# Windowed attention in a three-block kernel: attention weights turned in 32x32 blocks on VectorE and moved by transfers, the second tile's exponential with its row sum taken from PSUM, and a new order table

## The chip, the cores and the metric

The kernel runs on one core of a Trainium2 chip. The metric is the device time of one execution in microseconds (us); lower is better. Five instruction queues work side by side: PE (TensorE, matrix products and transposes; PEld is its weight load), DVE (VectorE), ACT (ScalarE), POOL (GpSimd) and SP (SyncE, which issues the transfers). Each queue runs its own instructions in the order in which they were written, and waits for the others through semaphores. TensorE's results land in PSUM, from which DVE and ACT read; everything else lies in SBUF, 128 partitions wide.

## The reference

The input is 16 sequences of 256 tokens with 128 channels. Four residual blocks follow each other: a state-space scan, a two-layer feed-forward block with local attention, a power attention, and the same feed-forward block once more.

```python
x = L0_attn_a_resid
x = x + scan_block(layernorm(x))
x = x + ffn_block(layernorm(x))
x = x + power_block(layernorm(x))
x = x + ffn_block(layernorm(x))
```

The change is in the feed-forward block. Each of its two layers is this, for each sequence (8 heads of 64, window of 64 tokens; a token sees its own window and the one before):

```python
h = shift_token(x)
q, k, v = split(h @ wqkv)              # to heads
q, k = l2norm(q) * qs, l2norm(k) * ksc
q, k = rotary_xpos(q, k)
sim = (8 * q) . k                      # per window, 64 queries by 128 keys
sim = where(mask, -max, sim)
attn = softmax(sim)
x = x + (attn . v) @ wo
h = layernorm(shift_token(x)) * lg + lb
a, g = split(h @ w1 + b1)
x = x + (a * gelu(g)) @ w2 + b2
```

## The kernel before, in words

All values are 32-bit floats. After the scan block (`ssm_block`), three blocks share one arena of SBUF (`mem`) and one set of PSUM banks: `ffn_block(1, ...)`, `power_block`, `ffn_block(3, ...)`. A block is a list of small steps, each with a place on one line of time: the place is counted in units of a planned length (39.2 for one turn of the feed-forward table, 20.5 for the power block's). At the end of `tile_hybrid_kernel` the three lists are laid one behind the other, where `ahead` says by how many units a block begins before the end of the one in front, sorted by place, and the steps are called in that order. Every engine is wrapped in `Pinned`, which keeps an engine's instructions in the written order; as all of them are issued from its one line, the profile gives L88 to nearly everything, and groups are told apart by tiles and shapes.

The feed-forward block has N = 32 sequence passes (two layers of 16 sequences), two in a group, so 16 groups. `period` is the order table of one turn: a word such as `we0.1:4` is the step `we` (weigh) on tile 0 of the second sequence of the group that entered 4 turns ago. A word without a point is a step of the whole group, in the feed-forward half of the layer (names with U). In one turn all steps of two sequences are issued once, each at its own lag.

The attention of one sequence, by steps (t is the tile of 128 queries; a is 0 for queries, 1 for keys; r is the half of the heads):

- `p`, `sq`, `ro`, `ss`, `ra`: queries and keys are projected (PE), squared (ACT), multiplied by the rotary tables (DVE), square-summed (DVE), and the two rotary parts added (`rotated`, POOL, two additions of half the width).
- `b`, `i`, `nw`: inverse norms `rn` (POOL and ACT). `no` (`normed`, POOL) multiplies q and k by them, four times a sequence.
- `t`, `tc`: queries and keys turned by PE, copied by ACT into `qkT`.
- `k` (`mask`, ACT) writes the band of 0 and -1e30 into a pair of PSUM banks, `s` (`scores`, PE) adds the products to it, `mx` (`maxima`, DVE) takes the row maxima of the 8 heads, `lm` (`less_maximum`, DVE) writes the difference to `pr` in SBUF and gives the pair back, `e` (`exponentials`, ACT) takes the exponential of 128 x 1024 in one instruction, `su` (`sums`, DVE) sums the rows and inverts, `wo` (`weights_of`, POOL) multiplies.
- `wt` (`turn_weights`, PE) turns the weights in four 128x128 transposes for each half into a PSUM bank, `wc` (`turned_weights`, ACT) copies the bank to `prT`, `we` (`weigh`, PE) multiplies the values by them.
- `oc`, `mi`, `ma`: the result is copied (ACT), multiplied by `wo` (PE) and added (DVE). After the second tile `ma` issues three transfers on SP, which write the token-shifted rows (`mem<-u_all`). `vc` (`values_out`) copies the values and issues two transfers on SP of 64 rows of 2 KB (`mem<-mem`), which make the copy of the values shifted by half a tile.

The feed-forward half of a group: `Us`, `Uf`, `Un` (layer norm), `Ut`, `Uc` (turned), `Ur` (six products with w1), `Ug` (three Gelu, with two loads of ACT's tables), `Um` (three products on DVE), `Ub`, `Ud` (w2), `Ua` (sum).

FFN_LATE names the buffers in the arena: a word count and how many of each. Attention weights have three `pr` and two `prT` buffers of 1024 words for each partition.

Of the kernel before, what the change touches and what calls it, by code (L numbers as in the profile page):

```python
# [20 lines left out]
P = 128  # L21
# [15 lines left out]
QK_SCALE = 8.0  # L37
MASKED = -1e30


# [5 lines left out]
def kernel(ctx: ExitStack, tc: tile.TileContext, io, out: bass.AP):  # L46
# [615 lines left out]
    NP = HEADS // 2  # L662
    HF = DH // 2
    NC = len(hidden_chunks())

    def ffn_weights(fw):
# [6 lines left out]
        for t in range(2):  # L673
            m = const.tile([P, P], F32, name=f"band{t}")
            pool.memset(m, 0.0)
            for w in range(t + 1):
                q0 = w * WINDOW
                part = m[q0 : q0 + WINDOW] if t else m

                for sign, base in ((1, 0), (-1, WINDOW)):  # L680
                    pool.affine_select(
                        out=part, in_=part, pattern=[[-sign if t == 0 else sign, P]],
                        compare_op=ALU.is_ge, fill=MASKED, base=base,
                        channel_multiplier=sign if t == 0 else -sign,
                    )
            bands.append(m)
# [55 lines left out]

    FFN_LATE = [("rn", 32, 2), ("qkT", 2048, 2), ("vx", 1536, 4), ("pr", 1024, 3), ("prT", 1024, 2), ("oT", 512, 2)]
    FFN_LATE += [("mx", 8, 4), ("rl", 8, 4), ("shifted0", 512, 1), ("shifted1", 512, 1), ("hn", 512, 1)]
    FFN_LATE += [("hnT", 512, 1), ("hid", 1536, 1), ("ub", 512, 1)]
    FFN_LATE += [(f"ln_{x}4", 4 * n, 4) for x, n in (("st", 6), ("mv", 2), ("r", 1), ("mr", 1))]

    def ffn_block(k, fw, store, shared):
# [112 lines left out]
        def rotated(n, q, t, a):  # L861
            m2 = q.pop(("m2", t, a))
            m = q["m", t, a] = sb.tile([P, HEADS, DH], F32, name=f"f{k}_m_{n}_{t}_{a}", tag="m", bufs=8)
            for x, y in ((slice(0, HF), slice(HF, DH)), (slice(HF, DH), slice(0, HF))):
                pool.tensor_add(m[:, :, x], m2[:, 0, :, x], m2[:, 1, :, y])
            sb.free(m2)
# [37 lines left out]
        def normed(n, q, t, a):  # L904
            m = q["m", t, a]
            pool.tensor_mul(m, m, q["rn"][:, t, a, :].unsqueeze(2).to_broadcast([P, HEADS, DH]))
            sb.free(q["rn"], 4)

# [50 lines left out]


        def maxima(n, q, t):
            mx = q["mx", t] = sb.tile([P, 2, NP], F32, name=f"f{k}_mx_{n}_{t}", tag="mx", bufs=4)
            dve.tensor_reduce(mx, q["sim", t], AX.X, ALU.max)

        def less_maximum(n, q, t):
# [4 lines left out]
        def exponentials(n, q, t):  # L970
            pr = q["pr", t]
            act.activation(pr, pr, AF.Exp)

        def sums(n, q, t):
            rl = q["rl", t] = sb.tile([P, 2, NP], F32, name=f"f{k}_rl_{n}_{t}", tag="rl", bufs=4)
            dve.tensor_reduce(rl, q["pr", t], AX.X, ALU.add)
            dve.reciprocal(rl, rl)
# [4 lines left out]

        def turn_weights(n, q, t, r):
            pr = q["pr", t]
            ppt = bank(q, ("ppt", t, r), [P, NP, P], f"f{k}_ppt_{n}_{t}_{r}")
            for p in range(NP):
                pe.transpose(ppt[:, p, :], pr[:, r, p, :], ident)
            sb.free(pr, 2)


        def turned_weights(n, q, t, r):
            if r == 0:
                q["prT", t] = sb.tile([P, 2, NP, P], F32, name=f"f{k}_prT_{n}_{t}", tag="prT")
            act.copy(q["prT", t][:, r], give_back(q, ("ppt", t, r)))

        def weigh(n, q, t):

            prT, vx = q.pop(("prT", t)), q["vx"]
            po = bank(q, ("po", t), [P, NP, P], f"f{k}_po_{n}_{t}")
            for p in range(NP):  # L1000
                for w in range(t + 1):
                    qs = slice(w * WINDOW, (w + 1) * WINDOW) if t else slice(0, P)
                    for r in range(2):
                        pe.matmul(
                            po[r * DH : (r + 1) * DH, p, qs], vx[:, 2 - w if t else 0, 2 * p + r, :],
                            prT[:, r, p, qs], start=True, stop=True,
                        )
            sb.free(prT)
            sb.free(vx, 2)
# [93 lines left out]
        def unit_sum(g, q):  # L1103
# [12 lines left out]
            nw=newton, no=normed, t=turn, tc=turned, k=mask, s=scores, mx=maxima, lm=less_maximum,  # L1116
            e=exponentials, su=sums, wo=weights_of, wt=turn_weights, wc=turned_weights, we=weigh,
            oc=weighed, mi=mix, ma=mixed, Us=unit_stats, Uf=unit_factors, Un=unit_norm, Ut=unit_turn,
# [3 lines left out]
        period = """  # L1122
            ns.0:0 Uf:5 p00.0:2 e1.1:4 ma0.0:4 ro01.0:2 t11.0:3 s0.0:3 tc11.0:3 ro11.1:3 oc1.0:4
            v0.0:2 sq00.0:2 su1.1:4 ra11.1:3 Ud0:6 vc0.0:2 Un:5 mx0.0:3 t10.0:3 wt00.1:4 ss00.0:2
            tc10.0:3 wt01.1:4 lm0.0:3 wc00.1:4 Ud1:6 ra01.0:2 wc01.1:4 i.1:3 mi1.0:4 n.0:1 wo1.1:4
            p11.0:2 ma1.0:4 Ua:6 v1.0:2 ro00.0:2 nw.1:3 sq11.0:2 k1.0:3 p10.0:2 ss01.0:2 ra00.0:2
            vc1.0:2 p00.1:2 ro11.0:2 Ut:5 no00.1:3 s1.0:3 Uc:5 no01.1:3 e0.0:3 we0.1:4 mx1.0:3
            ra11.0:2 sq10.0:2 nf.1:1 oc0.1:4 ut.0:1 wt10.1:4 ss10.0:2 wt11.1:4 lm1.0:3 wc10.1:4
            Ur10:5 uc.0:1 wc11.1:4 Ur11:5 ss11.0:2 e1.0:3 ro10.0:2 b.0:2 we1.1:4 no11.1:3 k0.1:3
            su0.0:3 ra10.0:2 t00.1:3 oc1.1:4 v0.1:2 tc00.1:3 su1.0:3 no10.1:3 t01.1:3 vc0.1:2  # L1130
            p01.1:2 sq00.1:2 wo0.0:3 Ur12:5 tc01.1:3 ss00.1:2 sq01.1:2 ro00.1:2 mi0.1:4 i.0:2 Ug:5
            wo1.0:3 s0.1:3 ma0.1:4 ro01.1:2 mi1.1:4 nw.0:2 Ur01:5 ma1.1:4 mx0.1:3 ra00.1:2 p10.1:2
            ss01.1:2 t10.1:3 Ub:5 sq10.1:2 Um1:5 t11.1:3 tc10.1:3 v1.1:2 lm0.1:3 tc11.1:3 no00.0:2
            wt00.0:3 vc1.1:2 wt01.0:3 no01.0:2 ss10.1:2 ns.1:0 wc00.0:3 p01.0:1 ro10.1:2 wc01.0:3
            no11.0:2 Ur00:5 k1.1:3 ra01.1:2 wt11.0:3 Um0:5 e0.1:3 wt10.0:3 Us:4 we0.0:3 n.1:1
            ra10.1:2 wc10.0:3 sq01.0:1 s1.1:3 oc0.0:3 su0.1:3 wc11.0:3 ut.1:1 p11.1:2 mx1.1:3
            wo0.1:3 Ur02:5 uc.1:1 Um2:5 t00.0:2 t01.0:2 no10.0:2 tc00.0:2 lm1.1:3 we1.0:3 sq11.1:2
            tc01.0:2 nf.0:0 mi0.0:3 ss11.1:2 k0.0:2 b.1:2
        """
# [372 lines left out]
    for block, length, ahead in (  # L1512
        (ffn_block(1, fw, False, shared), 39.2, 0.0), (power_block(w, dram, shared), 20.5, 60.0),
        (ffn_block(3, fw, True, shared), 39.2, 20.0),
    ):
        begin, work = block
        start = end - ahead
        line.append((start, begin, ()))
        line += [(start + at * length, step, args) for at, step, args in work]
        end = max(at for at, *_ in line)  # L1520
# [55 lines left out]
```

## Time and profile before

| what | value |
|---|---|
| median of 3 runs | 2166.41 us (2164.24 to 2166.89) |
| span of the profiled execution | 2164.0 us |
| mean granted TensorE clock in it | 0.982 |
| PE busy, share of the span | 2027.4 us, 94% |
| PEld | 1327.1 us, 61% |
| DVE | 1846.0 us, 85% |
| ACT | 1709.8 us, 79% |
| POOL | 1892.6 us, 87% |

Busy times are unions over the instructions of an engine; matmuls are pipelined and their ends modelled, so PE's busy time says that products follow each other without a gap, not that each runs at its peak. Successive instructions of ACT and DVE overlap a little, so a duration is longer than the distance from one start to the next; the distance is what a queue pays.

The chain that ended last, by engine: PE 55%, POOL 17%, DVE 9%, ACT 9%, issue 7%, the rest SP, DMA and queues. Some of the groups of the whole execution, by shape (busy us, mean ns of one):

| group | count | busy us | mean ns |
|---|---|---|---|
| PE transposes, bank<-ident,mem 128x128 (feed-forward and power block) | 3104 | 424.9 | 277 |
| ACT copies, mem<-bank 128x512 | 976 | 535.9 | 594 |
| ACT, mem<-mem 128x1024 (exponentials) | 224 | 238.2 | 1067 |
| DVE, mem<-pair,mem 128x1024 (less_maximum) | 128 | 155.6 | 1216 |
| DVE, sums mem<-mem 128x8 of 128x1024 | 128 | 152.8 | 1194 |
| POOL, mem<-mem 128x256 (rotated) | 512 | 360.6 | 729 |
| POOL, mem<-mem 128x512 | 320 | 329.5 | 1043 |

### The profile page before, as it was taken

To read this page: it belongs to the slowest core of one execution; us is meant where nothing else is said; L and a number is where in the kernel's file an instruction comes from. 1 tells how busy PE (TensorE), PEld (TensorE's weight loads), DVE (VectorE), ACT (ScalarE), POOL (GpSimd) and SP (SyncE) were. 2 spreads that over 40 slices of the span, in tenths; PEclk is the share of its full clock that TensorE was granted. 3 is DMA by queue.
4 is the path that set the end of the run, shared out by engine and by line. 5 is a ranking of instruction groups with operands and counts; after the bars stand their busy time and mean duration, and the time that the engine had idled before them with its cause. 6 is when DMAs were issued, how large, how long until landed. Compare 5 with 4: busy or idle time off the path is not lost.

```text
span 2164.0 us, 44300 instructions
## 1 busy us (share of the span) xinstructions
PE 2027.4 (94%) x16184; PEld 1327.1 (61%) x16184; DVE 1846.0 (85%) x3291; ACT 1709.8 (79%) x2879; POOL 1892.6 (87%) x2177
## 2 busy tenths in 40 slices
PE   6999999877999999999988999998899999999997
PEld 2344444334667677777765777775567777777775
DVE  3999999998988888888856999997988888888883
ACT  5777777746888887878866999997788887878874
POOL 6899999968999888888967999996999988888993
PEclk8999999999999999999997999999999999999999
DMA  3322322211110110111103323220010111101110
GB/s 100 98 84 78 103 80 77 83 44 24 24 23 16 23 24 18 22 23 23 23 11 118 112 87 119 105 95 8 21 23 17 23 23 24 23 16 33 28 28 23
DMA packets 96837, 104.35 MB, mean 48 GB/s; under 512 B 50818, under 2 KB 62956, under 8 KB 96620
## 3 DMA queue, kind: packets, MB, share of 16 engines
q1 hardware_dynamic: 95932, 101.37, 16.5%
q8 instruction: 128, 2.10, 0.4%
q14 instruction: 89, 0.73, 0.1%
q10 hardware_dynamic: 688, 0.15, 0.0%
HBM read 73.72 MB, written 2.62 MB: 35 GB/s over the span
## 4 chain that ended last, share of the span: by engine, by line
PE 55%; POOL 17%; DVE 9%; ACT 9%; issue 7%; SPq 1%; DMA 1%; POOLq 0%; DVEq 0%; ACTq 0%
PE bank L88 44%; POOL mem L88 7%; PE pair L88 7%; POOL bx L88 7%; DVE mem L88 6%; ACT mem L88 4%; DVE hs L88 2%; ACT pair L88 2%; SPq L88 1%; POOL hs L88 1%; ACT a L88 1%; DMA mem<-u_all 1%; PE xe_ps L88 1%; PE y_ps L88 1%; POOL sf L88 1%
## 5 line engine op out<-in xcount | busy, mean ns | idle before, releaser
L88 POOL TENSOR_TENSOR mem<-mem 128x256 f32<-128x256 f32 (+5 forms) x1328 | 1157.0, 901 | 88.0 <-DVE mem L88 66.2
L88 ACT COPY mem<-bank 128x512 f32<-128x512 f32 (+4 forms) x1152 | 592.4, 558 | 145.3 <-PE bank L88 139.9
L88 PEld LDWEIGHTS bank<-ident,mem 128*128 128x128 f32 x3104 | 352.4, 141 | 171.1 <-issue 105.3
L88 PE MATMUL bank<-ident,mem 128*128 128x128 f32 x3104 | 424.9, 277 | 15.7 <-POOL mem L88 11.0
L88 PE MATMUL bank<-wqkv,mem 128*128 128x512 f32 x768 | 384.8, 606 | 1.8 <-ACT mem L88 1.8
L88 DVE TENSOR_REDUCE mem<-mem 128x8 f32<-128x512 f32 (+1 forms) x384 | 325.9, 849 | 9.6 <-ACT mem L88 9.2
L88 DVE TENSOR_TENSOR mem<-bank,rope 128x1024 f32<-128x1024 f32 x256 | 309.1, 1217 | 25.1 <-POOL mem L88 16.6
L88 POOL TENSOR_TENSOR bx<-dx,bb 128x1024 f32<-128x1024 f32 x126 | 295.0, 2364 | 15.6 <-DVE dx L88 10.9
L88 DVE TENSOR_TENSOR_SCAN hs<-a,bx 128x1024 f32<-128x1024 f32 x128 | 291.7, 2284 | 14.0 <-ACT a L88 12.2
L88 ACT ACTIVATE mem<-mem 128x1024 f32<-128x1024 f32 (+2 forms) x384 | 281.0, 737 | 25.0 <-DVE mem L88 16.7
L88 PE MATMUL pair<-mem 64*64 64x128 f32 (+2 forms) x4096 | 256.6, 296 | 22.9 <-DVE mem L88 13.9
L88 PE MATMUL y_ps<-hs,ident 128*128 128x512 f32 x512 | 243.3, 600 | 11.0 <-DVE hs L88 6.5
L88 PEld LDWEIGHTS pair<-mem 64*64 64x64 f32 (+2 forms) x4096 | 194.7, 160 | 75.2 <-issue 27.7
L88 ACT ACTIVATE a<-delta,neg_a 128x510 f32<-128x510 f32 x256 | 176.3, 690 | 76.8 <-DVE hs L88 71.8
L88 ACT ACTIVATE mem<-bank 128x512 f32<-128x512 f32 (+1 forms) x272 | 160.9, 593 | 61.7 <-PE bank L88 57.8
L88 PE MATMUL bank<-mem 128*64 128x64 f32 (+2 forms) x4608 | 203.3, 255 | 5.4 <-ACT mem L88 2.9
L88 PEld LDWEIGHTS bank<-mem 128*64 128x64 f32 (+1 forms) x4608 | 156.8, 128 | 64.3 <-issue 30.0
L88 PE MATMUL bank<-mem,w 128*128 128x512 f32 x384 | 191.9, 598 | 3.8 <-ACT mem L88 3.8
L88 PEld LDWEIGHTS y_ps<-hs,ident 128*128 128x128 f32 x512 | 95.7, 190 | 148.7 <-issue 120.3
L88 DVE TENSOR_REDUCE mem<-pair 128x8 f32<-128x1024 f32 x128 | 153.3, 1198 | 30.3 <-PE pair L88 30.3
L88 PEld LDWEIGHTS bank<-wqkv,mem 128*128 128x128 f32 x768 | 128.6, 194 | 72.3 <-issue 60.7
L88 DVE TENSOR_TENSOR mem<-pair,mem 128x1024 f32<-128x1024 f32 x128 | 155.6, 1216 | 0.4
(135 smaller groups left out, 2830.4 us busy)
## 6 DMA issues: line engine op xcount, KB each, us to landing
bb<-repsd SPq DMA_DIRECT2D x128, 256.0 KB
mem<-pngd SPq DMA_DIRECT2D x64, 512.0 KB
mem<-mem SPq DMA_DIRECT2D x128, 128.0 KB
mem<-u_all SPq DMA_DIRECT2D x64, 64.0 KB
mem<-u_all SPq DMA_DIRECT2D x64, 63.5 KB
x_all<-in_resid_dram SPq DMA_DIRECT2D x8, 256.0 KB
out_dram<-x_all SPq DMA_DIRECT2D x8, 256.0 KB
wqkv<-in_wqkv_dram SPq DMA_DIRECT2D x6, 256.0 KB
```

What stands on the lines that cost most here:

```text
L88: bi = getattr(self.eng, name)(*args, **kw)
```

## The change

In the feed-forward block:

- The weights are no longer turned by PE and copied by ACT. DVE transposes each tile of weights in blocks of 32x32 (`turn_weights`, one instruction of 128 x 1024 for each tile) into a buffer `T`, ordered by block column. A block transpose leaves each block in its own 32 partitions, so a step `mv` (`move_weights`) issues 16 transfers on SP for each sequence, each of 32 partitions by 2 KB, which put the blocks where they belong, into `PT`. `weigh` reads `PT` in runs of 32 columns. `T` and `PT` hold both tiles of a sequence, two buffers of 2048 words each; `prT` is gone.
- For the second tile (RAW = (1,)) the queries aren't multiplied by their inverse norms. `maxima` multiplies the maxima by the negated norms, and 8 exponentials of 128 x 128 read the scores in PSUM, with the norm as scale, the scaled maximum as bias and the row sum as a second output; `less_maximum` and the sum on DVE fall away for this tile, and the pair of banks is given back after its exponentials. Its mask fill is -1e25 instead of -1e30.
- `rotated` is one addition of the whole width that reads its second part with the halves exchanged, instead of two of half the width.
- The order table is a new one: the steps stand in other places and at other lags. A turn's planned length is 35.6 units instead of 39.2, and the last block begins 60 units before the end of the power block instead of 20.

```diff
+FAR = -1e25
+RAW = (1,)
+QB = 32
...
+    NB = P // QB
+    NORMED = 3
...
-    FFN_LATE = [("rn", 32, 2), ("qkT", 2048, 2), ("vx", 1536, 4), ("pr", 1024, 3), ("prT", 1024, 2), ("oT", 512, 2)]
+    FFN_LATE = [("rn", 32, 4), ("qkT", 2048, 2), ("pr", 1024, 3), ("T", 2048, 2), ("vx", 1536, 4), ("PT", 2048, 2)]
...
-            for x, y in ((slice(0, HF), slice(HF, DH)), (slice(HF, DH), slice(0, HF))):
-                pool.tensor_add(m[:, :, x], m2[:, 0, :, x], m2[:, 1, :, y])
+            pool.tensor_add(
+                m.rearrange("p h (f d) -> p h f d", f=2), m2[:, 0].rearrange("p h (f d) -> p h f d", f=2),
+                m2[:, 1].rearrange("p h (f d) -> p h f d", f=2)[:, :, ::-1],
+            )
...
+        def query_norms(q):
+            return q["rn"][:, 1, 0].rearrange("p (c r) -> p r c", r=2)
+
         def maxima(n, q, t):
             mx = q["mx", t] = sb.tile([P, 2, NP], F32, name=f"f{k}_mx_{n}_{t}", tag="mx", bufs=4)
             dve.tensor_reduce(mx, q["sim", t], AX.X, ALU.max)
+            if t in RAW:
+                dve.scalar_tensor_tensor(mx, mx, -1.0, query_norms(q), ALU.mult, ALU.mult)
...
         def exponentials(n, q, t):
-            pr = q["pr", t]
-            act.activation(pr, pr, AF.Exp)
+            if t not in RAW:
+                pr = q["pr", t]
+                act.activation(pr, pr, AF.Exp)
+                return
...
+            for r in range(2):
+                for p in range(NP):
+                    act.activation(
+                        pr[:, r, p, :], sim[:, r, p, :], AF.Exp, bias=mx[:, r, p : p + 1],
+                        scale=norms[:, r, p : p + 1], accum_out=rl[:, r, p : p + 1],
+                    )
+            ps.give_pair_back(q, ("sim", t))
...
-        def turn_weights(n, q, t, r):
-            pr = q["pr", t]
-            ppt = bank(q, ("ppt", t, r), [P, NP, P], f"f{k}_ppt_{n}_{t}_{r}")
-            for p in range(NP):
-                pe.transpose(ppt[:, p, :], pr[:, r, p, :], ident)
-            sb.free(pr, 2)
-
-
-        def turned_weights(n, q, t, r):
-            if r == 0:
-                q["prT", t] = sb.tile([P, 2, NP, P], F32, name=f"f{k}_prT_{n}_{t}", tag="prT")
-            act.copy(q["prT", t][:, r], give_back(q, ("ppt", t, r)))
+        def turn_weights(n, q, t):
+            if t == 0:
+                q["T"] = sb.tile([P, NB, 2, HEADS, QB], F32, name=f"f{k}_T_{n}", tag="T")
+            dve.transpose(
+                q["T"][:, :, t],
+                sb.free(q.pop(("pr", t))).rearrange("p r c (b i) -> p b (r c) i", i=QB),
+            )
+
+
+        def move_weights(n, q):
+            turned_, dst = q.pop("T"), sb.tile([P, NB, 2, HEADS, QB], F32, name=f"f{k}_PT_{n}", tag="PT")
+            q["PT"] = dst
+            for b in range(NB):
+                for kb in range(NB):
+                    sp.dma_start(dst[kb * QB : (kb + 1) * QB, b], turned_[b * QB : (b + 1) * QB, kb])
+            sb.free(turned_)
...
+                    bs = slice(2 * w, 2 * w + 2) if t else slice(0, NB)
...
                         pe.matmul(
-                            po[r * DH : (r + 1) * DH, p, qs], vx[:, 2 - w if t else 0, 2 * p + r, :],
-                            prT[:, r, p, qs], start=True, stop=True,
+                            po[r * DH : (r + 1) * DH, p, qs].rearrange("d (b i) -> d b i", i=QB),
+                            vx[:, 2 - w if t else 0, 2 * p + r, :], PT[:, bs, t, r * NP + p, :],
+                            start=True, stop=True,
                         )
...
+            k0.1:3 mi1.0:4 sq10.1:2 ma1.0:4 Ur11:6 ut.0:1 vc0.0:2 v1.0:2 Us:5 tc10.1:3 vc1.0:2
+            Ur10:6 ra01.1:2 no01.0:2 no11.0:2 s0.1:3 Ur12:6 ro10.1:2 uc.0:1 Ug:6 tr0.0:3 p00.0:1
+            ss10.1:2 sq00.0:1 Ur01:6 no11.1:3 mx0.1:3 su1.0:3 no00.0:2 t00.0:2 t01.0:2 ra00.1:2
+            lm0.1:3 Um1:6 Uf:5 Ur00:6 wo1.0:3 p11.1:2 ns.0:0 nf.0:0 tc00.0:2 ro00.0:1 nf.1:1
+            tr1.0:3 mv.0:3 p01.0:1 t10.0:2 tc01.0:2 ra10.1:2 k0.0:2 sq11.1:2 ss11.1:2 ss00.0:1
+            e0.1:3 b.1:2 t11.0:2 tc11.0:2 n.0:0 s0.0:2 tc10.0:2 mx0.0:2 ra00.0:1 Um0:6 n.1:1
+            lm0.0:2 we0.1:4 t11.1:3 sq01.0:1 tc11.1:3 ro01.0:1 v0.1:2 i.1:2 k1.1:3 p10.0:1
+            we1.1:4 oc0.1:4 v1.1:2 Un:5 su0.1:3 nw.1:2 p11.0:1 ro11.1:2 s1.1:3 ra01.0:1 no01.1:2
+            ss01.0:1 ra11.1:2 ut.1:1 no00.1:2 mx1.1:3 oc1.1:4 vc0.1:2 e0.0:2 mi0.1:4 wo0.1:3
+            ma0.1:4 sq11.0:1 vc1.1:2 mi1.1:4 sq10.0:1 su0.0:2 uc.1:1 ma1.1:4 Ur02:6 Ub:6
+            ro11.0:1 ra11.0:1 p00.1:1 Um2:6 e1.1:3 ro10.0:1 k1.0:2 ss10.0:1 su1.1:3 ss11.0:1
+            ra10.0:1 we0.0:3 p01.1:1 Ud0:6 t00.1:2 oc0.0:3 sq00.1:1 tr0.1:3 Ut:5 Uc:5 tc00.1:2
+            s1.0:2 sq01.1:1 t01.1:2 b.0:1 wo1.1:3 ss00.1:1 tc01.1:2 we1.0:3 i.0:1 Ud1:6 oc1.0:3
+            mx1.0:2 e1.0:2 ro01.1:1 v0.0:1 t10.1:2 ro00.1:1 wo0.0:2 mi0.0:3 tr1.1:3 ns.1:0
+            mv.1:3 nw.0:1 ma0.0:3 p10.1:1 ss01.1:1 Ua:6
...
-        (ffn_block(1, fw, False, shared), 39.2, 0.0), (power_block(w, dram, shared), 20.5, 60.0),
-        (ffn_block(3, fw, True, shared), 39.2, 20.0),
+        (ffn_block(1, fw, False, shared), 35.6, 0.0), (power_block(w, dram, shared), 20.5, 60.0),
+        (ffn_block(3, fw, True, shared), 35.6, 60.0),
```

## The prediction

> **What bounds the kernel now.** I read the page first (span, busy slices), then the table of windows over single turns of the feed-forward loop, then the timelines of PE, DVE and SP inside one turn, and last the groups by shape.
>
> ```profile
> span 2164.0 us, 44300 instructions
> PE   6999999877999999999988999998899999999997
> ...
> ```
>
> PE is at nine tenths nearly everywhere, so the page alone doesn't tell the stages apart. By the names of the tiles the feed-forward blocks run from 490 to about 1130 us and from about 1500 to the end; the scan block before them and the power block between them keep their instructions. Inside a feed-forward block the trace repeats every 39.08 us, which is one turn of the table (two sequences). Columns: busy time of each engine, then granted clock, DMA share, GB/s.
>
> ```profile
> core 0: us, PE busy (x) PEld busy (x) DVE busy (x) ACT busy (x) POOL busy (x), PEclk, DMA share, GB/s
> 800.36:839.44 39.08, 39.08 (x359) 27.98 (x358) 33.59 (x49) 31.65 (x55) 33.71 (x45) 1.00 0.10 22
> 839.44:878.52 39.08, 39.08 (x359) 27.99 (x358) 33.61 (x49) 31.68 (x55) 33.70 (x45) 1.00 0.10 22
> ```
>
> PE never rests; DVE, POOL and ACT have 5.5, 5.4 and 7.4 us to spare. So a turn is PE's work, and each block has 16 turns plus a start and an end.
>
> ```profile
> 777.77 1.47 PE L88 MATMUL bank<-ident,mem 128*128 128x128 f32 x12
> 779.08 1.50 PE L88 MATMUL bank<-w,mem 128*128 128x128 f32 x12
> ...
> 773.39 2.35 DVE L88 TENSOR_TENSOR mem<-bank,rope 128x1024 f32<-128x1024 f32 x2
> ...
> 791.11 1.21 DVE L88 TENSOR_REDUCE mem<-mem 128x8 f32<-128x1024 f32 x1
> 792.35 0.20 DVE L88 RECIPROCAL mem<-mem 128x8 f32<-128x8 f32 x1
> 792.47 1.17 DVE L88 TENSOR_REDUCE mem<-mem 128x8 f32<-128x1024 f32 x1
> ```
>
> Prices from start to start: a transpose on PE (779.08 - 777.77) / 12 = 0.109 us; a 1024-element DVE operation 2.35 - 1.22 = 1.13; a sum with the reciprocal that waits for it 1.24 + 0.12.
>
> **The change, part by part, in one turn.**
>
> **PE.** turn_weights gives up 4 transposes for each of 2 tiles, 2 halves and 2 sequences: 32 x 0.109 = 3.49 us. weigh issues the same matmuls, but reads its moving side in pieces of 32 (four pieces, or two). The start of a matmul bounds a piece's price: 32 matmuls of 64 columns take 1.08 us, 16 of 128 take 1.02, so 0.004 us is left besides the columns; 160 extra pieces are at most 0.6 us, at least 0. I take 0: PE 39.08 - 3.49 = 35.6 (to 36.2).
>
> **ACT.**
>
> ```profile
> L88 ACT COPY mem<-bank 128x512 f32<-128x512 f32 x144 | 79.8, 592 | 18.5 <-PE bank L88 18.3
> L88 ACT ACTIVATE mem<-mem 128x32 f32<-128x32 f32 x24 | 5.8, 242 | 0.4
> L88 ACT ACTIVATE mem<-bank,lb,lg 128x512 f32<-128x512 f32 x6 | 4.7, 781 | 5.9 <-PE bank L88 5.9
> ...
> L88 ACT COPY mem<-bank 128x128 f32<-128x128 f32 x32 | 7.2, 291 | 0.0
> ```
>
> turned_weights goes: 8 copies at 0.49 from start to start (three take 1.57), 3.9 us. Two exponentials of 1024 elements go, at 0.95: 1.9. In come 16 exponentials of 128 elements from PSUM, with bias and scale columns and a row sum. The copy of that size takes 0.291, two columns cost 0.781 - 0.592 = 0.19: 0.48 each, or 0.37 where it overlaps the next by the 0.105 that the copies do. No row shows the row sum. Below: nothing, 0.37. Above: no overlap and a separate instruction like the smallest here, 0.48 + 0.24 = 0.72. I take 0.45, nearer to the lower end, as DVE's accumulator read (82 ns in the power block) lies under the next operation: 7.2 us. ACT 31.7 - 5.8 + 7.2 = 33.1 (31.9 to 37.4).
>
> **DVE.** The second tile loses its subtraction (2 x 1.13) and its sum (2 x 1.24), and gains a product of 8 elements that waits for the maximum, priced like the reciprocal (2 x 0.24): 29.3 us. Then 4 block transposes of 1024 elements. None is in the trace. Nearest are the one-pass operations of this size, 1.13; below, 0.68 as for a 512-element reduction; above, 2.28, the scan's price for 1024. I take 1.13: DVE 33.9 (32.1 to 38.5).
>
> **POOL.** The second tile's query scaling goes (2 x 0.95) and eight pairs of half additions become single ones (2 x 0.69 - 0.95 = 0.43 each): 33.7 - 5.3 = 28.4; if the reversed reading eats that gain, 31.8. It stays clear of the bound. The other fill value of the mask and the larger rn buffer issue nothing in the loop.
>
> **SP.** move_weights issues 16 transfers for each sequence, each 32 rows of 2 KB.
>
> ```profile
> 781.93 4.65 SPq L88 DMA_DIRECT2D mem<-u_all  x3
> 786.68 1.20 SPq L88 DMA_DIRECT2D mem<-mem  x2
> ...
> 764.08 1.80 SPq L88 DMA_DIRECT2D mem<-mem  x2
> ...
> q1 hardware_dynamic: 179, 0.27, 66.9%
> ```
>
> The nearest transfers are vx's (64 rows of 2 KB): 0.56 us each to issue, 0.61 apart, and once 1.15 (the 1.80 less 0.65), behind the u_all group. So 32 x 0.61 = 19.5 us, with the 2 x (4.65 + 1.2) that are there: 31.2 of 35.6 us. The last line is of the 1.7 us in which one such transfer moves: 0.669 x 1.7 x 16 / 128 rows = 0.142 us a row, so one move is 512 x 0.142 / 16 = 4.5 us of the DMA engines, less than its issue. A move lands about 16 x 0.61 + 2 = 12 us after the second block transpose. Queued behind it on SP are vc's, ma's transfers and the next move. By places in the new table the tightest run is tr1.1 (0.95 of a turn) to we0.0 (1.76): 0.81 x 35.6 = 28.8 us, in which SP must issue move 1 (9.8), ma1.0 (4.65), vc1.0 (1.2), move 0 (9.8) and land it (2): 27.5. That fits by 1.3 us. What is late when it doesn't is we0.0, and PE stands behind it.
>
> Here a rule speaks against the change. The Trainium skill (DMA: Bandwidth & Descriptors, Bandwidth) says to batch transfers to 1 MiB and gives 0.95 us for 64 KB, measured from HBM over the other path. Were that a time that each of 32 moves holds the queue, an estimate from that page is 30.4 us, and SP would need 42 us a turn, past today's 39.08; by the rows it needs 31.2.
>
> **Outside the turns.** The third block may start 40 table units earlier: at 1460 to 1500 us DVE leaves some 10 us idle and PE 8; I take -8 (0 to -15). Against it, all Ur, Ug and Um go from lag 5 to 6, past the last attention: one more chain of gate, product and fall at each block's end, half hidden under the power block; +8 (0 to +20). Together 0.
>
> **Sum.** PE's 35.6 stands against 33.9, 33.1 and 31.2 on engines that feed each other in order, 95, 93 and 88% full where they were 86, 81 and 30. I add 0.8 us of waits: 36.4 (a choice; 0 to 1.8). Gain 32 turns x (39.08 - 36.4) = 86 us. The profiled execution has a span of 2164.0; the median of the runs is 2166.4, 2.4 above. 2164 - 86 + 2.4 = 2080.
>
> **Rivals.**
> 1. A wait takes the old bound's place: SP's run tr1.1 to we0.0 fails by 2.5 us (a few issues at 1.15 instead of 0.56 do it, and they follow the u_all group as here). PE waits in every turn: 38.1, 2164 - 32 x 1.0 + 2 = 2135. For it: a margin of 1.3 us. Against: PT has two buffers and the table can slip.
> 2. DVE or ACT becomes the bound: block transposes at the scan's 2.28 give 38.5, 2164 - 18 + 2 = 2148; ACT at 0.72 gives 37.4, 2112. For it: neither operation is in the trace. Against: both lie at far ends.
> 3. Slower: SP's issue itself bounds the loop. From (39.08 - 11.7) / 32 = 0.86 us a transfer, gap included, it decides; at the 1.15 seen once and 0.06 between, 32 x 1.21 + 11.7 = 50.4 us a turn, 2164 + 32 x 11.3 + 2 = 2528. For it: one issue in four shown took that long. Against: that one stood behind 127-row transfers, and rows drain faster than they are issued.
>
> **Chances.** Forecast 0.55 (its own range 2045 to 2115: turns of 35.6 to 37.4, ends within 15 us); rival 1 0.14; rival 2 0.11; rival 3 0.15; about no change 0.05, where rivals 1 and 2 meet the old turn; of this, 0.02 is faster by more than 0.2% (4 us, about what a measurement of this kernel can tell from no change), 0.02 within it and 0.01 slower. Faster is 0.55 + 0.14 + 0.11 + 0.02 = 0.82, same 0.02, slower 0.16. The range for 8 in 10 reaches from 2040 (PE's full 111 us and the earlier start) to 2170, so that it takes in rivals 1 and 2; left out are rival 3 with the slower hundredth and some 0.03 below, 0.19.
>
> **What would show it.** A turn of 35.6 to 37 us with PE still full, and 32 fewer transposes in it, is the forecast. Block transposes near 1.2 us, small exponentials 0.4 to 0.5 us apart, DVE's and ACT's busy shares above 90%: steps right. PE idle before the first weigh of a sequence, released by a DMA: rival 1. DVE or ACT full and PE not: rival 2. SP issuing without a break, over 0.86 us each: rival 3. The forecast is wrong if a turn is over 37.4 us, or if the ends cost more than 20 us.

## The result, and the profile after

| | median | runs | profiled span | mean clock |
|---|---|---|---|---|
| before | 2166.65 us | 2164.24 to 2167.72 (4) | 2164.0 us | 0.982 |
| after | 2283.80 us | 2273.46 to 2287.44 (4) | 2278.9 us | 0.947 |

The ratio is 1.0538, with a 95% interval of 1.0512 to 1.0564: the changed kernel is 117 us slower, where 86 us of gain were forecast. It lies outside the range, on the other side.

The page of after first: span, PE's share in 40 slices, the chain that ended last, and the one group of PE that stands out (counts, busy us, mean ns, then idle time just before it and what ended most of that).

```profile
span 2278.9 us, 43705 instructions
...
PE   6999999868889899898868999998779899899877
...
PE 44%; POOL 12%; ACT 10%; DVE 10%; SPq 10%; issue 8%; DMA 5%; POOLq 0%; ACTq 0%; DVEq 0%
...
L91 PE MATMUL bank<-mem 128*64 128x64 f32 (+2 forms) x4608 | 225.7, 268 | 147.8 <-DMA mem<-mem 137.6
```

PE, at 9 throughout the loops before, is now at 8 in many slices. 137.6 us of its idle time stand before the products that read the moved weights (`weigh`), and a transfer ends them. SP's queue and the DMA, 1% each of the chain before, are 15% of it.

The windows over four turns of the first feed-forward block (columns as in the prediction):

```profile
core 0: us, PE busy (x) PEld busy (x) DVE busy (x) ACT busy (x) POOL busy (x), PEclk, DMA share, GB/s
760.00:800.90 40.90, 37.79 (x328) 25.53 (x327) 33.97 (x50) 32.41 (x76) 30.69 (x34) 0.96 0.30 72
...
841.80:882.70 40.90, 37.58 (x327) 25.48 (x326) 33.97 (x50) 32.41 (x76) 30.64 (x34) 0.96 0.30 72
```

A turn takes 40.9 us where it took 39.08, and no engine fills it: DVE, ACT and POOL have 7 to 10 us to spare, PE over 3, and PE's clock is 0.96. So the bound is a chain through several queues. It shows when the timelines of SP, PE and DVE over one turn are laid side by side. SP (start, time from the first of the run to the end of the last, how many issues):

```profile
849.00 10.06 SPq L91 DMA_DIRECT2D mem<-mem  x16
859.16 4.66 SPq L91 DMA_DIRECT2D mem<-u_all  x3
863.94 13.43 SPq L91 DMA_DIRECT2D mem<-mem  x20
877.47 4.60 SPq L91 DMA_DIRECT2D mem<-u_all  x3
889.88 2.46 SPq L91 DMA_DIRECT2D mem<-mem  x4
```

PE:

```profile
873.59 1.02 PE L91 MATMUL bank<-wqkv,mem 128*128 128x512 f32 x2
877.94 1.97 PE L91 MATMUL bank<-mem 128*64 128x128 f32 x16 [3.32 <-DMA mem<-mem]
...
883.84 1.10 PE L91 MATMUL pair<-mem 64*64 64x128 f32 x32
```

DVE:

```profile
885.01 1.22 DVE L91 TENSOR_REDUCE mem<-pair 128x8 f32<-128x1024 f32 x1 [3.26 <-PE pair L91]
886.27 0.17 DVE L91 SCALAR_TENSOR_TENSOR mem<-mem 128x8 f32<-128x8 f32 x1
886.35 2.35 DVE L91 TENSOR_TENSOR mem<-bank,rope 128x1024 f32<-128x1024 f32 x2
888.62 1.23 DVE L91 STREAM_TRANSPOSE mem<-mem 128x1024 f32<-128x1024 f32 x1
```

From 849.00 SP issues without a pause: the 16 transfers of move 1, the three of `ma1.0`, the two of `vc1.0`, the 16 of move 0 (the row of 20 ends with two of `vc1.1`). The last of move 0 is issued at 875.51; at 877.94 the first `weigh` of the turn (`we0.0`) starts, after 3.32 us in which PE had nothing and which a `mem<-mem` transfer ends. Behind it on PE stand projections and turns, then the scores (`s1.0`, 883.84). DVE waits 3.26 us for them, takes their maximum, does three operations in its written order and transposes (`tr1.1`, 888.62, done at 889.85). At 889.88 SP begins the next move 1. The chain closes: 877.94 - 849.00 = 28.94 us by way of SP, 889.88 - 877.94 = 11.94 us back by way of PE and DVE, 40.88 together. This is the turn.

Within the way back lies a second loss. The same turn in four windows, cut at the end of PE's work, at `we0.0`, and 3.4 us later:

```profile
866.00:874.60 8.60, 8.60 (x92) 5.26 (x90) 8.24 (x13) 7.69 (x21) 8.07 (x11) 1.00 0.49 122
874.60:877.90 3.30, 0.01 (x1) 0.00 (x0) 3.30 (x6) 2.45 (x9) 2.79 (x3) 1.00 0.45 111
877.90:881.30 3.40, 3.36 (x18) 2.44 (x19) 1.76 (x3) 1.08 (x2) 3.32 (x4) 0.50 0.28 63
881.30:892.00 10.70, 10.70 (x126) 8.88 (x125) 6.73 (x9) 7.89 (x25) 6.25 (x9) 1.00 0.09 20
```

After the wait PE runs at half its clock for 3.4 us, which costs 1.7 us of work: PE's work is 35.9 (the turn of the kernel without transfers, below), and 35.9 + 3.3 + 1.7 = 40.9, the turn.

### The profile page after: what moved, and what is told of

Same layout as the page of the kernel before. It is cut to its first block, busy times and chain, and to the rows that moved or that the text cites. A ratio compares the mean times of both kernels' runs of the same rounds, so it can differ in the third digit from the quotient of the medians.

```text
span 2278.9 us, 43705 instructions
## 1 busy us (share of the span) xinstructions
PE 1988.5 (87%) x15160; PEld 1254.1 (55%) x15160; DVE 1866.0 (82%) x3355; ACT 1734.7 (76%) x3583; POOL 1795.3 (79%) x1857
## 4 chain that ended last, share of the span: by engine, by line
PE 44%; POOL 12%; ACT 10%; DVE 10%; SPq 10%; issue 8%; DMA 5%; POOLq 0%; ACTq 0%; DVEq 0%
PE bank L91 35%; SPq L91 10%; DVE mem L91 7%; PE pair L91 6%; POOL bx L91 6%; ACT mem L91 6%; DMA mem<-mem 4%; POOL mem L91 2%; DVE hs L91 2%; ACT pair L91 2%; POOL hs L91 1%; PE y_ps L91 1%; ACT a L91 1%; PE xe_ps L91 1%; POOL sf L91 1%
## 5 line engine op out<-in xcount | busy, mean ns | idle before, releaser
L91 POOL TENSOR_TENSOR mem<-mem 128x512 f32<-128x512 f32 (+3 forms) x1008 | 1062.2, 1073 | 245.0 <-ACT mem L91 114.9
L91 ACT COPY mem<-bank 128x512 f32<-128x512 f32 (+4 forms) x896 | 452.7, 545 | 179.5 <-PE bank L91 168.0
L91 PE MATMUL bank<-wqkv,mem 128*128 128x512 f32 x768 | 415.3, 647 | 27.0 <-ACT mem L91 24.7
L91 PE MATMUL bank<-mem 128*64 128x64 f32 (+2 forms) x4608 | 225.7, 268 | 147.8 <-DMA mem<-mem 137.6
L91 PE MATMUL bank<-ident,mem 128*128 128x128 f32 x2080 | 301.1, 283 | 13.2 <-ACT mem L91 6.6
L91 PEld LDWEIGHTS bank<-ident,mem 128*128 128x128 f32 x2080 | 238.5, 144 | 117.1 <-issue 75.7
L91 PEld LDWEIGHTS bank<-mem 128*64 128x64 f32 (+1 forms) x4608 | 176.1, 136 | 227.5 <-issue 132.1
L91 DVE TENSOR_REDUCE mem<-mem 128x8 f32<-128x512 f32 (+1 forms) x320 | 245.1, 775 | 54.0 <-ACT mem L91 53.5
L91 ACT ACTIVATE mem<-pair,mem 128x128 f32<-128x128 f32 x512 | 226.5, 466 | 24.0 <-DVE mem L91 24.0
L91 ACT ACTIVATE mem<-mem 128x1024 f32<-128x1024 f32 (+2 forms) x320 | 212.9, 670 | 5.0 <-POOL mem L91 2.3
```

The costliest lines, as they stand in the source:

```text
L91: bi = getattr(self.eng, name)(*args, **kw)
```

## The experiments

A time is that of one run where no number of runs or interval is given, beside the kernel before on the same chip; "turn" is the usual distance between the Gelu groups of two turns in the middle of a block.

### The kernel after without the transfers

```diff
-            turned_, dst = q.pop("T"), sb.tile([P, NB, 2, HEADS, QB], F32, name=f"f{k}_PT_{n}", tag="PT")
-            q["PT"] = dst
-            for b in range(NB):
-                for kb in range(NB):
-                    sp.dma_start(dst[kb * QB : (kb + 1) * QB, b], turned_[b * QB : (b + 1) * QB, kb])
-            sb.free(turned_)
+            q["PT"] = q.pop("T")
```

> The changed kernel without any of the 1024 transfers of the moves: weigh reads T in place of PT, so that blocks stand in the wrong partitions. Theory (the turn is a loop: 27 us in which SP issues without a break from the end of block transpose tr1.1 to the last transfer of move 0, 1.8 us to land, 12 us on PE and DVE back to the next tr1.1): without the moves PE sets the turn again, 35.6 to 36.6 us, no granted clock below 1 inside the turns, and 2060 to 2110 us in all. Rival A (DVE, ACT and POOL at 93 to 95% hold each other up): the turn stays above 38 us. Rival B (ends of the blocks cost on their own, through the deeper lags): the turn falls to 36, but the total only to some 2130.

Measured: 2099.97 us (before 2168.74). The windows of two turns:

```profile
800.00:835.60 35.60, 35.60 (x322) 24.08 (x319) 34.48 (x51) 32.26 (x77) 30.49 (x34) 1.00 0.11 24
835.60:871.20 35.60, 35.60 (x322) 24.08 (x320) 34.47 (x51) 32.25 (x77) 30.53 (x34) 1.00 0.11 23
```

PE is full again, although DVE is 97% full. The windows are cut at 35.6 us by hand; the turn itself, from one `we0.0` to the next, is 35.9 us:

```profile
843.14 1.09 PE L91 MATMUL bank<-mem 128*64 128x128 f32 x16
...
879.01 1.09 PE L91 MATMUL bank<-mem 128*64 128x128 f32 x16
```

All the other edits do inside the turns nearly what they should (35.6 us were reckoned); the transfers are what undoes it. But PE's saving is 32 x (39.08 - 35.88) = 102 us, and 2168.7 - 102 = 2067: some 33 us of it don't arrive even without transfers. They come up again below.

### The last block transpose and its move earlier

```diff
-            mx1.0:2 e1.0:2 ro01.1:1 v0.0:1 t10.1:2 ro00.1:1 wo0.0:2 mi0.0:3 tr1.1:3 ns.1:0
-            mv.1:3 nw.0:1 ma0.0:3 p10.1:1 ss01.1:1 Ua:6
+            tr1.1:3 mv.1:3 mx1.0:2 e1.0:2 ro01.1:1 v0.0:1 t10.1:2 ro00.1:1 wo0.0:2 mi0.0:3 ns.1:0
+            nw.0:1 ma0.0:3 p10.1:1 ss01.1:1 Ua:6
```

> One change in the order table: tr1.1 and mv.1 stand before mx1.0 instead of eight words later, so that block transpose and move no longer wait on DVE behind a maximum that needs PE's scores behind we0.0. Theory: the way back in the loop (12 us) is cut, SP starts move 1 about 6 us earlier against PE, no wait of PE for the move remains, the turn is 35.6 to 37 us and the total 2070 to 2130 us. Rival A (engines too full): no change of the turn, 40.9 us. Rival C (SP's 33 us of issue in a turn are the bound as such, whatever the order): the turn falls by less than 2 us.

Measured: 2149.95 us (before 2168.74), turn 36.2 to 37.1 in the first block. One of its turns:

```profile
845.66 1.09 PE L91 MATMUL bank<-mem 128*64 128x128 f32 x16 [1.14 <-DMA mem<-mem]
```

The SP run is not shorter (move 1 begins at 851.87, `we0.0` at 881.95); only the way back is cut, as `tr1.1` no longer stands behind the maximum of the scores that wait for `we0.0`. PE's wait shrinks from 3.3 us to 2 at most (none was expected to remain), and its clock stays full in the steady turns. The turn came as expected; the total misses its range by 20 us, which therefore lie outside the steady turns.

### The row copy in 112 and 15 partitions

```diff
-                sp.dma_start(h[1:, i : i + 2, HD:], u2[: P - 1, :, HD:])
+                sp.dma_start(h[1:113, i : i + 2, HD:], u2[:112, :, HD:])
+                sp.dma_start(h[113:, i : i + 2, HD:], u2[112 : P - 1, :, HD:])
```

> The shifted copy of 127 rows is issued as 112 and 15 rows, nothing else. Theory: the 3.1 us issue behind it comes from the 127 rows going through one DMA engine; split, the group of u_all transfers takes some 2.6 us instead of 4.66, SP's unbroken run is 2 us shorter, and the turn falls from 40.9 to 38.5 to 39.2 us, the total by 65 to 90 us to 2190 to 2215. Rival A: SP's time falls, the turn stays at 40.9. Rival D (the long issue has another cause than the 127 rows): the group still takes 4.6 us and nothing moves.

Measured: 2216.88 us (before 2168.74), turn 38.2 on the mean of nine in the first block. SP's run in one of its turns:

```profile
837.71 10.07 SPq L91 DMA_DIRECT2D mem<-mem  x16
847.89 2.98 SPq L91 DMA_DIRECT2D mem<-u_all  x4
850.99 13.16 SPq L91 DMA_DIRECT2D mem<-mem  x20
```

Four issues take 2.98 us where three took 4.66, in the same place: shorter by 1.7 us with one issue more. This is the other half of the loop, and cutting it helps as well: of 40.9 us, 1.7 go by this, and part of the half-speed time too. The turn is 0.3 us under its range, the total 2 us above. The Trainium skill (DMA: Bandwidth & Descriptors, "Why a DMA increments its semaphore by 16 and not by 1") has a rule that fits: a transfer is spread over the largest number of engines up to 16 that divides its partitions, 1 for 127, and by the same rule 16 for 112 and 15 for 15. No run here shows which engines a transfer used. That the split shortens the issues is shown; that the one engine is the reason is argued.

### The first move ahead of rows and values

```diff
-            if t == 1:
+            if t == 1 and n % GS == 1:
+                shift(n, q)
+        def shift(n, q):
...
-            tr1.0:3 mv.0:3 p01.0:1
+            tr1.0:3 mv.0:3 sh.0:4 hv.0:2 p01.0:1
```

The transfers of `ma1.0` and `vc1.0` become steps of their own (`sh`, `hv`) behind move 0; the same for `vc`'s two.

> The transfers of ma1.0 and vc1.0 are issued behind move 0 instead of between move 1 and move 0; the arithmetic stays where it is. Theory: move 0 follows move 1 at once or when its block transpose is done, 4 us earlier, the loop is 4 us shorter and the turn about 36.8 us, total 2120 to 2160. Rival A: the turn stays at 40.9. Rival C (SP's issue as such): the same number of issues, so no change either.

Measured: 2156.66 us (before 2168.74).

```profile
828.00:863.90 35.90, 35.90 (x328) 24.38 (x328) 34.67 (x51) 32.55 (x77) 30.49 (x34) 1.00 0.33 80
863.90:899.80 35.90, 35.90 (x328) 24.37 (x328) 34.72 (x51) 32.51 (x77) 30.53 (x34) 1.00 0.34 82
```

The moves 1 and 0 on SP now follow each other, and `we0.0` starts without a wait:

```profile
859.44 22.84 SPq L91 DMA_DIRECT2D mem<-mem  x32
...
883.92 1.09 PE L91 MATMUL bank<-mem 128*64 128x128 f32 x16
```

The run is 24.5 us instead of 28.9 (859.44 to 883.92), PE is full again and the turn 35.9 in most cases, better than expected, as the half-speed time goes too. The number of transfers has not changed, and their issue is no cheaper (0.71 us each here); only who stands behind whom on SP has.

### Split rows and first move ahead

The last two edits together.

> The two SP edits together: the 127-row copy as 112 and 15 rows, and the transfers of ma1.0 and vc1.0 behind move 0. With the second alone PE was already without a wait in the turns (35.9 us), so the loop theory expects the turn to stay at 35.9 us, and only the turns at the ends of the blocks, which wait for moves, to lose some us: 2135 to 2150 us. If SP's time still counted inside the turns (rival C), the turn would fall further and the total to some 2110.

Measured: 2144.50 us (before 2167.49), turn 35.9 in most cases, as expected.

### The same, with half of the moves at the ends on ACT's queue

```diff
-                    sp.dma_start(dst[kb * QB : (kb + 1) * QB, b], turned_[b * QB : (b + 1) * QB, kb])
+                    q_ = act if (n < 2 or n >= N - 4) and kb % 2 else sp
+                    q_.dma_start(dst[kb * QB : (kb + 1) * QB, b], turned_[b * QB : (b + 1) * QB, kb])
```

> As the kernel before this one, and for the first 2 and last 4 of 32 sequence passes of a block ACT's queue issues half of the 16 transfers of each move. Theory for what is lost at the ends (in the last turns there is too little other work to hide a move's 10 us of issue, so PE waits and its clock halves): each move there takes 5 us instead of 10, the last turns of both blocks shorten by 8 to 15 us each, 2110 to 2135 us in all. Rival: the ends are long because the new table needs one turn more from first projection to last Gelu, and moves hardly matter there: within 5 us of the kernel before this one.

Measured: 2182.11 us (before 2167.49): a miss, slower by 38 us than without the edit. Of these, 22 us arise before the first Gelu of the blocks (15.5 in the first, 6.8 in the last) and 16 between the first and the last Gelu of each; the turn in which the last passes begin takes 44.1 us, where it took 33.3 and 31.8. ACT waits 13.1 us for `mem<-mem` transfers before 660 us and 23.6 us between 1040 and 1180 us, where it had no such wait without the edit. It runs in its written order, so that its exponentials and copies stand behind its issues and their waits; halving SP's queue does not pay for that.

### The third block begins 20 instead of 60 units early

```diff
-        (ffn_block(3, fw, True, shared), 35.6, 60.0),
+        (ffn_block(3, fw, True, shared), 35.6, 20.0),
```

It stands on the kernel with the first move ahead (2156.66).

> The kernel with the transfers of ma1.0 and vc1.0 behind move 0 (2156.7 us in one run), but with the third block begun 20 units before the end of the power block, as before the change, instead of 60. If the earlier start was worth what it was given (8 us), this takes 2162 to 2168 us; if it collides with the power block's end, it takes 2156 or less.

Measured: 2165.35 us (the kernel before took 2167.49 on this chip and 2168.74 on that of the 2156.66), 8.7 us more, one run of each. The total is in the range expected, but half of it is chance. Up to the end of the first block both kernels issue the same instructions in the same order, and there this one is already 4.8 us later (its last Gelu at 1152.1 us, against 1147.3). From that Gelu to the last one of all it takes 998.4 us, against 994.5: by the traces the earlier start is worth about 4 us, half of the 8 that were counted for it.

### PE kept busy before the first weigh

```diff
+        def warmed(n, q):
+            pb = bank(q, "warm", [P, 512], f"f{k}_warm_{n}")
+            for _ in range(6):
+                pe.matmul(pb, ident, weights(n)["wq"][:, :512], start=True, stop=True)
+            give_back(q, "warm")
...
-            ra10.0:1 we0.0:3 p01.1:1
+            ra10.0:1 wm.0:3 we0.0:3 p01.1:1
```

The kernel after, with six products that nobody reads.

> The changed kernel with 6 products of 128x512 more in each turn, 2.6 us of PE's time, right before the first weigh of the group's first sequence, where PE waits 3.3 us for the move; their result is not read. If the halved clock for 3.4 us after that wait is caused by PE's idling, the clock stays at 1 in the steady turns and a turn takes about 1.7 us less in spite of the added work: 39.0 to 39.6 us, 2220 to 2250 us in all. If the clock has another cause, the turn stays at 40.9 us or grows, 2279 us or more.

Measured: 2279.39 us (before 2167.49); in a steady turn:

```profile
801.00:842.00 41.00, 41.00 (x338) 26.61 (x337) 33.98 (x50) 32.44 (x76) 30.74 (x34) 1.00 0.31 73
```

The clock is 1.00 in every steady turn: what halves it is PE's idling, not the transfers. But the turn is as long as before, since each product takes two PE instructions here, and the six take 5.2 us instead of the 2.6 that I had reckoned: 35.9 + 5.2 = 41.1, so that PE itself now fills it. The expectation on the time fails by my price, so the case was run again with three.

### The same with three products

The edit above with `range(3)`.

> The kernel after, with three idle 128x512 products (2.6 us as they were measured) ahead of the first weigh of each pass instead of six. Theory: the granted clock halves because PE waits about 3.3 us for the moves; with a wait of about 0.7 us left it stays at 1.00, and a turn is the loop of SP and DVE without the 1.7 us of half speed: 39.0 to 39.6 us; total 2215 to 2240. Rival: the halving hangs on the moves' own transfers, or a short wait is enough for it: turn 40.5 us or more, total 2265 or more. Rival: the loop is longer than I counted: turn 40 to 41 at a clock of 1.00.

Measured: 2252.38 us median (2248.21 to 2256.79), ratio 1.0396 (1.0378 to 1.0415).

```profile
816.00:856.00 40.00, 38.54 (x331) 25.53 (x330) 34.00 (x51) 32.46 (x77) 30.67 (x34) 1.00 0.31 73
856.00:895.00 39.00, 37.83 (x329) 25.14 (x328) 33.29 (x50) 31.77 (x76) 30.67 (x34) 1.00 0.30 73
895.00:934.00 39.00, 38.39 (x331) 25.53 (x330) 33.84 (x51) 32.31 (x77) 30.70 (x34) 1.00 0.31 75
```

The turn is 39.4 on the mean (nine turns in 355 us), the clock 1.00, and PE idles 0.6 to 1.6 us before `we0.0` in the first block. Three products more than the kernel needs make it faster by 31 us. The loop can be read at full clock here, from move 1 to `we0.0` and on to the next move 1:

```profile
848.79 10.60 SPq L91 DMA_DIRECT2D mem<-mem  x16
...
878.14 1.09 PE L91 MATMUL bank<-mem 128*64 128x128 f32 x16 [1.17 <-DVE mem L91]
...
888.48 10.16 SPq L91 DMA_DIRECT2D mem<-mem  x16
```

The way back is 10.3 us (878.14 to 888.48); from after, 11.94 - 1.7 = 10.2. So the loop of after at full clock is 28.9 + 10.2 = 39.1, and the half-speed time was the other 1.7. The turn being in its range, the 12 us by which the total is above its own lie outside the steady turns.

### All three mends of the order

Split rows, first move ahead, and the last block transpose earlier.

> The kernel after, with all three edits: row copy split in 112 and 15, the transfers of the second sequence's rows and values behind the first move, and the last block transpose with its move earlier in the turn. Theory: the two edits before it have already freed PE inside the turns (35.9 us), so the third brings nothing there: turn 35.6 to 36.0; it can help only at the ends, where a last move is waited for: total 2130 to 2148. Rival: DVE's earlier transpose holds up the maximum and the exponentials that stand behind it: 2150 to 2165.

Measured: 2141.17 us median of 4 (2139.20 to 2141.64), before 2165.56; ratio 0.9881 (0.9868 to 0.9895). The turn is 36.1 to 37.0, longer than without the third edit and than the 35.6 to 36.0 expected; the total is as expected.

### Split rows and first move ahead, more rounds

> The split rows and the first move ahead of the other transfers, once more, with more rounds for the interval: 2140 to 2149, that is 0.988 to 0.992 of the kernel before; if the earlier 2144.5 was a chance, 2150 to 2160.

Measured: 2143.14 us median of 5 (2138.01 to 2147.00), ratio 0.9893 (0.9876 to 0.9909). The two versions aren't told apart; both beat the kernel before, by 1.1 to 1.2%. 36 us of it, about one turn:

```profile
792.00:828.00 36.00, 36.00 (x325) 24.39 (x324) 34.77 (x51) 32.66 (x77) 30.56 (x35) 1.00 0.34 84
```

### A control: the kernel before with split rows

> A control: the kernel before, with its row copy split in 112 and 15 rows. Theory: there SP isn't on the path inside the turns, so shorter issues change nothing there; turn 39.08, total within 6 us of the kernel before, 2160 to 2170. Rival: the slow copy costs that kernel too, at the ends or by its own landing: 2150 or less.

Measured: 2155.43 us median of 4 (2155.12 to 2157.30), ratio 0.9951 (0.9936 to 0.9966): 10 us faster, between the two expectations. The turns are 39.1 as before. The gain lies at the ends of the blocks: from the first to the last Gelu the first block is 4.6 us shorter and the last 5.3. At the end of the first block DVE waits for these copies (6.7 us from 1075 us on, 0.9 in the control). SP at the end of the first block, before and in this control:

```profile
1091.82 40.53 SPq L88 DMA_DIRECT2D mem<-u_all  x12
```

```profile
1090.63 36.56 SPq L88 DMA_DIRECT2D mem<-u_all  x16
```

So of the 24 us by which the mended kernel beats the one before, 10 can be had by the split alone. Against the control the change, with its order mended, is worth 2155.4 - 2141.2 = 14 us.

## Why the prediction was wrong, point by point

**What bounds the kernel before: right.** Without transfers a turn follows PE's work, with PE full, to 35.9 us; 35.6 were reckoned.

**The prices: mostly right.** The groups by shape over two turns of after:

```profile
L91 POOL TENSOR_TENSOR mem<-mem 128x512 f32<-128x512 f32 x32 | 36.3, 1158 | 1.7 <-DVE mem L91 1.4
...
L91 POOL TENSOR_TENSOR mem<-u_all,b 128x512 f32<-128x512 f32 x2 | 2.5, 1268 | 0.0
...
L91 ACT ACTIVATE mem<-pair,mem 128x128 f32<-128x128 f32 x32 | 14.2, 466 | 1.0 <-DVE mem L91 1.0
...
L91 DVE STREAM_TRANSPOSE mem<-mem 128x1024 f32<-128x1024 f32 x8 | 9.9, 1234 | 0.0
...
L91 ACT ACTIVATION_READ_ACCUMULATOR mem<-pair,mem 128x1 f32 x32 | 6.8, 214 | 0.0
```

| term | taken | measured |
|---|---|---|
| PE, a turn's work | 35.6 us | 35.88 |
| DVE | 33.9 | 34.0 to 34.5 |
| ACT | 33.1 | 32.3 to 32.4 |
| POOL | 28.4 (to 31.8) | 30.5 to 30.7 |
| small exponential, start to start | 0.45 | 0.44 (eight starts from 846.26 to 849.32) |
| block transpose of 1024, start to start | 1.13 | 1.16 (1.23 long) |
| one issue of a move | 0.61 | 0.63 (10.06 for 16) |

Extra pieces in `weigh` cost nothing that can be seen: from start to start 0.064 us for a product of 128 columns and 0.034 for one of 64, before and without transfers alike. The 0.3 us by which PE's turn is longer lies with other products, most of it with the 24 projections (10.80 us a turn from start to start, 10.42 before). POOL is the one that was mis-sized: the merged addition takes 1.26 to 1.28 us, 1.24 from start to start (0.95 was taken), so eight of them give back 2 us of what the merging was to save. That its second part is read with the halves exchanged isn't the reason: the addition `mem<-u_all,b`, which reads straight on, takes the same 1.27 us above, and 1.28 before the change:

```profile
L88 POOL TENSOR_TENSOR mem<-u_all,b 128x512 f32<-128x512 f32 x32 | 40.8, 1276 | 2.2 <-DVE x_all L88 2.2
```

The 0.95 came from rows of 1.04 us, and those are products that repeat one value along a head. POOL isn't the bound, and nothing follows from it.

**"That fits by 1.3 us": here the forecast failed.** The place was right, the SP run from `tr1.1` to `we0.0`. The run was nearly right: 27.5 us were reckoned, 28.9 measured, and the 1.4 us between them alone use up the margin of 1.3. What was wrong is what it was held against. The 28.8 us available were read from places in the new table (0.95 to 1.76), that is, 0.19 of a turn or 6.8 us were left for the way from `we0.0` back to the next `tr1.1`. But places only say who is issued ahead of whom. That way is itself a chain: PE's work up to the scores, the maximum, three operations of DVE, the transpose; it takes 10.2 us at full clock, and the prediction did not add it up. The run and the way back depend on each other in turn, so their sum is the least turn, 28.9 + 10.2 = 39.1: 3.5 us over the 35.6, of which the way back is 3.4 (10.2 - 6.8) and the run 1.4, less the margin of 1.3. Three things show it, each by one end of the loop: taking the way back apart (36.2 to 37.1), shortening the run by 1.7 us (38.2), and reordering the run (24.5 us of it left, turn 35.9).

**Rival 1 had the mechanism and not its price.** It let the run fail by 2.5 us and forecast 38.1 a turn. The least turn is 39.1; and the wait that comes with it has a price of its own that no term had, 1.7 us of work lost at half clock: 40.9. Three idle products take that price away again (39.4). In after, 20 waits of 2.2 to 4.4 us stand before `we0.0` in the middle of the two blocks, and 19 of them were followed by 3.4 us at a clock of 0.50 (two of them by 6.8); one of 2.9 us was not. With split rows 6 of 20 were, in the same place, the shortest of them 1.75 us, while others of up to 2.8 us were not. So no single length divides them in these runs; all of 3.1 us or more were followed by it. The Trainium skill (TensorE: Matmul & The Clock Gate, Part 1) has the halving and the 3.4 us, and puts the fall after an idle window of about 3.4 us; here shorter waits sufficed, though not each time.

**Rivals 2 and 3 fall.** DVE and ACT have over 6 us to spare in after, and without the transfers PE, not DVE, sets the turn. SP's issues cost 0.63 us each (0.71 with the first move ahead) and not 0.86; SP waits some 8 us a turn for DVE (57.0 us between 700 and 1000 us), so that its rate as such isn't the bound. In the mended kernel it issues the same transfers in a turn of 35.9. The rule on batching of the prediction, with its 42 us a turn, is not borne out by these small transfers between partitions: they are cheaper to issue than its figure. That the result lies near it is by another mechanism.

**"Outside the turns together 0": wrong by 40 to 140 us.** The earlier third block is worth about 4 us by the traces (8 taken). The 8 for the later Ur, Ug and Um was put at the ends; the table shows the loss at the starts, for which the sum had no term. PE's loss in each stretch, worked out from the trace as idle time plus half of the time at half clock (us):

| stretch | before | no transfers | all mends | after |
|---|---|---|---|---|
| first block, first projection to third Gelu | 16 | 40 | 41 | 61 |
| its next nine turns | 0 | 0 | 2 | 47 |
| to its last Gelu | 13 | 13 | 30 | 42 |
| last block, first projection to third Gelu | 17 | 40 | 39 | 63 |
| its next nine turns | 0 | 2 | 1 | 49 |
| to its last Gelu | 12 | 3 | 20 | 33 |
| sum | 58 | 98 | 133 | 295 |

PE's saving is 102 us by the turns, 111 as reckoned. Less the growth of the sum, that leaves 62 to 71 us without transfers, 27 to 36 with all mends and -135 to -126 in after; measured are 69, 24 and -117, so the table accounts for the times to within some 10 us of the nearer bound. Three parts are told apart. First, each block's start loses 22 to 25 us more than before, without the transfers and with them in the mended kernel. Second, at the ends, where there is little other work for PE, the moves themselves are waited for: (30 - 13) + (20 - 3) = 34 us in the mended kernel. Third, in the kernel as changed the loop takes its 96 us inside the 18 steady turns, and some 69 us more at starts and ends than the mended one; there too PE waits for moves (11.0 us in the first start, 20.3 at the end of the first block).

What PE waits for in a start, from 490 us to the first Gelu, before and without transfers (us in total, times, longest; two rows of each):

```profile
PE bank L88 <- ACT mem L88: 2.0, 3, 0.9
PE pair L88 <- ACT pair L88: 1.6, 2, 0.9
```

```profile
PE bank L91 <- ACT mem L91: 11.7, 8, 2.6
PE pair L91 <- ACT pair L91: 7.3, 6, 2.4
```

and at the end of the first block of the kernel with all mends:

```profile
PE bank L91 <- DMA mem<-mem: 13.9, 4, 4.6
```

In the start it is ACT that PE waits for more than before, in the end the moves. What makes ACT late in the start, one of the new lags or its new exponentials, wasn't tried; that stays open.

## What to carry to other kernels

A wait that "fits" on one queue is not yet safe in a loop: follow the chain from the waiting instruction on until it comes back to the one that feeds the queue, add up the times along it, and hold that sum against the turn; places in an order table say who stands ahead of whom, not how long the way is. When an engine's work is replaced by transfers, look first at what else stands on the issuing queue between the data and its reader: putting the urgent transfers ahead and splitting one 127-row copy took the same change from 5.4% slower to 1.1% faster. And measure a saving in steady turns and in starts and ends apart, as a pipeline that is made deeper gives part of it back at each end.

## What the runs showed of the hardware that was not expected

- Waits of PE of 2.2 to 4.4 us cost 1.7 us more than themselves in 19 of 20 turns, by 3.4 us at half clock; no single length of the wait decided it. Filling most of the wait with products that nobody reads made the kernel 31 us faster.
- A row sum taken with an exponential from PSUM is a second instruction of ACT (214 ns on the mean), but it overlaps its neighbours: 0.44 us from one exponential of 128 to the next, 466 ns being the length of one.
- A copy of 127 partitions holds up the issues behind it on SP: three issues in 4.66 us, four in 2.98 once it is cut into 112 and 15, and that alone made the kernel before 0.5% faster.
- On POOL an addition of 128x512 takes 1.26 to 1.28 us, with the halves of one input exchanged or not; an operation of that size in which one value is repeated along a head takes 1.04.
